# Two attention-and-feed-forward blocks on one core: cross-attention's first scores in whole steps, a last division two steps nearer, and the first mixture slot placed ahead of the last unit's norm

## The chip, the core and the metric

The kernel runs on one core of a Trainium2 chip. A core has five engines with a queue of instructions each: TensorE (PE; its weight loads are listed apart as PEld), VectorE (DVE), ScalarE (ACT), GpSimd (POOL) and SyncE (SP), which here issues most DMAs. Instructions of one engine start in the order of its queue, and wait for other engines by semaphores. Matmul results go to eight banks of PSUM; a bank can be written again when its reader is done. The metric is the device time of one execution in microseconds (us); a profiled execution adds the start and end of every instruction, and the share of full speed that TensorE's clock was granted.

## The reference, cut to what matters

Two blocks follow each other on x, 2 x 1024 tokens of width 256, 16 heads of 16:

```python
# block 0
q = _ln(latents); x = latents + _mha(q, q)                 # self-attention, 1024 keys
x = x + _mha(_ln(x), _ln(ctx))                             # cross-attention, 64 keys
h = _ln(x)                                                 # mixture: 8 experts, the best 2
vals, idx = top_k(h @ rw.T + rb, 2); gates = softmax(vals)
x = x + sum(gates * (gelu(h @ fc1[idx]) @ fc2[idx]))       # 256 -> 1024 -> 256
# block 1
x = x + softmax(q k^T * 0.25) v @ proj                     # self-attention, 1024 keys
x = x + softmax(q kc^T * 0.25 + bias(mask)) vc @ proj      # cross-attention, 64 keys, masked
x = x + gelu(_ln(x) @ fc1.T) @ fc2.T
```

All is in float32. Every softmax subtracts the row's maximum.

## The kernel before, in words

**Layers, cells, units.** A layer is one block. Its self-attention is written out as 128 cells: 2 batches x 8 steps "h" (two halves of the queries times four groups of four heads) x 8 blocks of 128 keys. A cell of `self_attention` computes, for four heads side by side in TensorE's rows, the scores of block "b" with the maxima subtracted (L969; ScalarE makes the exponentials, L947), and ten cells ahead the scores "a" from which VectorE takes the maxima (L937, four reduces of 128 x 512). Every one or two cells `product` (L1024) multiplies the exponentials with the values; ScalarE copies the result (L1036) and GpSimd adds it up (L1037). In the last ten cells there are no scores "a" left; then `maxima[0]` is false, and `helper()` gives such additions and other small work to VectorE instead of GpSimd.

A **unit** is 512 tokens; there are four in a layer. When a unit's self-attention is finished (`finish`), its row sums are inverted, turned through DRAM, spread and multiplied (`invert`, `turn_out`, `spread_out`, `divide` at L568, at set cells), and the projection (`project`, L492) is added to x. Then come, as tasks of a planner (`Stream`): the norm for cross-attention (`cnorm`, L381 to L412, L424), its queries (`ask`, L1295), its attention (`weigh`), its projection (`share`), and in layer 0 the mixture's `dispatch_task` of the unit: norm, router, top-2 choice, places, and eight indirect DMAs on GpSimd that scatter the rows by expert (L1676).

**The planner.** In each cell it advances "light" tasks by one step, up to a budget of about 1.1 us of assumed TensorE time, and in odd cells heavier tasks up to 2.2 us. A step says by `yield` how much TensorE time it takes (positive) or how long to wait until the next (negative). If more than 1.2 us of an odd cell stay free, the product of the cell before is made alone. After the last cell `rest` goes on by assumed time and rank. These figures only set the order in which instructions are written for TensorE, VectorE, ScalarE and SP; GpSimd's order is made by a scheduler.

**`weigh`.** While scores "a" still run (units 0 and 1 of each layer) it is a chain of 22 cells: eight half steps of first scores (`scores`, L1337, two banks each, two token tiles of four, with two reduces of 128 x 256 at L1345), `parts` (L1358) after each four, then `largest` (the maxima turned by TensorE, L1364), `weights` (scores again, minus the maxima, L1374 and L1380, exponentials L1385), `product` with the values and with ones for the sums, and the division through DRAM as above (`inverted`, `sent`, `brought`, `divided`, L1427). In layer 1 each bank begins with a matmul that adds the mask. Units 2 and 3 take another path, with whole steps and the division on TensorE (`undivided` L1434 and L1444, `division` L1459).

**The handover.** After layer 0's cells the experts' "slots" (256 rows of one expert: L1926 turns the rows, L1961 and L1967 the first layer, L1992 the second) begin. Slot 0 needs units 0 and 1 to be dispatched (`find(2)`, then `rows(2)`), slots 1 to 4 unit 2 (`find(3)`, `rows(3)`), the others unit 3. `find` searches on VectorE which expert and which rows a slot has; `load` issues weights (L1864) and rows (L1856) on the SP queue. Beside them run the keys and values of layer 1's context (L1207 to L1248), the last heads of unit 3 put together on TensorE (`side_by_side`, L880 to L906), and units 2 and 3 of cross-attention.

Of the kernel before, what the change touches and what calls it, by code (L numbers as in the profile page):

```python
# [51 lines left out]
P = 128  # L52
B, S, D, H, DH = 2, 1024, 256, 16, 16
SK = 64
# [181 lines left out]
def two_blocks(  # L236
# [17 lines left out]
    const = ctx.enter_context(tc.tile_pool(name="const", bufs=1))  # L254
# [24 lines left out]
    weights = {}  # L279
# [87 lines left out]
    maxima = [True]  # L367
# [213 lines left out]
    def self_attention(layer, tail, heads, arrive, extra, when_ready, beside=None):  # L581
# [7 lines left out]
        pools = ExitStack()  # L589
# [33 lines left out]
        QB, mx = {}, {}  # L623
# [217 lines left out]
        def finish(h, cell):  # L841


            b, qh, g = h // 8, h // 4 % 2, h % 4
            if g == 0:
                ot[b, qh] = opool.tile([P, 2, 512], F32, tag="ot", name=f"ot_{names}{b}{qh}")
            if layer == 0 and h >= 8 * B - 2:

                if g == 3:
                    stream.add(  # L850
                        side_by_side([acc.pop(h - 1), acc.pop(h)], ot[b, qh][:, 1, :]), 2.0,
                        mark="compact", rank=80,
                    )
                    project(b, qh, ["compact"])
                return
            if g % 2 == 0:
                sm = small.tile([P, 32], F32, tag="sums", name=f"sums_{names}{h}")
                sums[g // 2] = next_heads(), sm
            n, sm = sums[g // 2]
            dst = ot[b, qh][:, g // 2, :]  # L860
            send(acc.pop(h), n, g % 2, sm)
            if g % 2 == 1:
                by = opool.tile([P, 512], F32, tag="by", name=f"by_{names}{h}", bufs=1)
                gather(n, dst)
                slow = maxima[0]
                at_cell(cell + 1, lambda: invert(n, sm))
                at_cell(cell + 1 + slow, lambda: turn_out(n, sm))
                at_cell(cell + 2 + slow, lambda: spread_out(n, by))

                late = 3 + 2 * slow  # L870
                at_cell(cell + late, lambda: divide(dst, by))
                if g == 3:
                    at_cell(cell + late + 1, lambda: project(b, qh))
# [434 lines left out]
    def weigh(layer, b, pool, w, name, held):  # L1308
# [4 lines left out]
        q = held["ot"]  # L1313
        pts, pairs = {}, {}
        whole = maxima[0]
        mx = pool.tile([P, 2, 4, 4, 2], F32, tag="mxc", name=f"mx_{name}")
        turned_mx = []

        def scores(g, n, t0=0, nt=4):

            got = [(r, *bank()) for r in (2 * n, 2 * n + 1)]
            for r, _, p in got if layer == 1 else ():
                at = slice(32 * r, 32 * r + 1)
                nc.tensor.matmul(
                    p[:, : nt * P].rearrange("p (c k) -> p c k", k=SK),
                    lhsT=ones[at, :].bitcast(F32R),
                    rhs=mask_f[at, b * SK : (b + 1) * SK]
                    .bitcast(F32R)
                    .unsqueeze(1)
                    .to_broadcast([1, 2 * nt, SK]),  # L1330
                    start=True,
                    stop=False,
                )
            for t in range(nt):
                for r, _, p in got:
                    rows = slice(32 * r, 32 * r + 32)
                    nc.tensor.matmul(  # L1337
                        p[:, t * P : (t + 1) * P],
                        lhsT=q[rows, g, (t0 + t) * P : (t0 + t + 1) * P],
                        rhs=kbd[rows, g, b].rearrange("p u k -> p (u k)"),  # L1340
                        start=layer == 0,
                        stop=layer == 0 or t == nt - 1,
                    )
            for r, i, p in got:
                nc.vector.tensor_reduce(  # L1345
                    mx[:, g, r, t0 : t0 + nt, :].rearrange("p t u -> p (t u)"),
                    p[:, : nt * P].rearrange("p (c k) -> p c k", k=SK),
                    AX.X, ALU.max, negate=True,
                )
                free.append(i)  # L1350
# [119 lines left out]
        extra = 0.2 * layer  # L1470
        if whole:

            costs = {scores: 0.5 + extra / 2, largest: 0.9, weights: 1.1, product: 1.75}
            cells = [[] for _ in range(22)]
            for k in range(8):
                g, n, half = k // 4, k // 2 % 2, k % 2
                cells[k].append((scores, g, n, 2 * half, 2))
                if k % 4 == 3:
                    cells[k].append((parts, g))
            cells[9].append((largest,))  # L1480
            for g in range(2):
                for n in range(2):
                    cells[10 + 3 * g + (1 + g) * n].append((weights, g, (2 * n, 2 * n + 1)))
                at = 12 + 4 * g
                for after, step in ((0, product), (2, inverted), (2, sent), (3, brought), (5, divided)):
                    cells[at + after].append((step, g))
            for now in cells:
                for step, *args in now:
                    step(*args)
                us = sum(costs.get(step, 0.0) for step, *_ in now)  # L1490
                if us and now is cells[-1]:
                    yield us, None, True
                elif us:
                    yield us, 0.0
                elif now is not cells[-1]:
                    yield 0.0
            return
        costs = {scores: 1.0 + extra, largest: 0.9, weights: 1.2, undivided: 1.9, division: 0.55}
# [56 lines left out]
    def dispatch_task(unit, pool, counted):  # L1555
# [44 lines left out]
        mx = small.tile([P, 2, 4], F32, tag="mx2", name=f"mx2_{name}")  # L1600
        hots = [pool.tile([P, 4, E], F32, tag=f"hot{k}", name=f"hot{k}_{name}") for k in range(2)]
        for k in range(2):
            hot = hots[k]
            nc.vector.tensor_reduce(mx[:, k, :], lg, AX.X, ALU.max)
            nc.vector.tensor_tensor(hot, lg, mx[:, k, :].unsqueeze(2).to_broadcast(shape), ALU.is_equal)
            nc.vector.tensor_tensor(hot, hot, desc_b, ALU.mult)
            first = small.tile([P, 4], F32, tag="first", name=f"first_{name}{k}")
            nc.vector.tensor_reduce(first, hot, AX.X, ALU.max)
            nc.vector.tensor_tensor(hot, desc_b, first.unsqueeze(2).to_broadcast(shape), ALU.is_equal)
            yield -1.0  # L1610
            if k == 0:
                nc.vector.scalar_tensor_tensor(lg, hot, -3.0e38, lg, ALU.mult, ALU.add)
                nc.vector.tensor_scalar(
                    xd[:, :, D + M_E0], first, -1.0, float(E), ALU.mult, ALU.add
                )
# [17 lines left out]
        else:  # L1633
# [9 lines left out]
            pk, lhsT=ones, rhs=before.rearrange("p e t -> p (e t)"), start=False, stop=True  # L1643
# [20 lines left out]
        at = small.tile([P, 2, 4], U32, tag="at", name=f"at_{name}")  # L1664
        for k in range(2):
            mine = small.tile([P, 4, E], F32, tag="mine", name=f"mine_{name}{k}")
            nc.vector.tensor_tensor(mine, hots[k], place.rearrange("p e t -> p t e"), ALU.mult)
            nc.vector.tensor_reduce(at[:, k, :], mine, AX.X, ALU.max)
            yield -0.5
        counted()  # L1670

        for t in range(4):
# [133 lines left out]
    class Mixture:  # L1806
# [211 lines left out]
        def find(self, units):  # L2018

            last = units == len(NFULL)  # L2020
            had = self.places[-1].tiles if self.places else None
            end = NSLOT if last else NFULL[units]
            n = end - (self.ends[-1] if self.ends else 0)
            if units == 2:
                self.caps = expert_tiles("2", (FULL, ANY))
                caps = 2 * self.caps[:1]
            else:

                caps = [self.caps[last], *expert_tiles(f"{units}", (OVER, ANY) if last else (FULL,))]
            yield -0.9  # L2030
            pool = self.epool[1] if self.epool else const
            places = Places()
            yield from places.make(pool, f"{units}", n, had, caps, last)
            self.places.append(places)
            self.ends.append(end)
            yield 0.3
            yield -3.0

            self.load(1)
# [141 lines left out]
    def block(layer, tail, heads=None, beside=None):  # L2181

        pools = {}
# [6 lines left out]
        if layer == 0:  # L2190
            open_pools()
            context_places(0, pools["cpool"])
            choice(0, pools["cpool"])
            bias_out.extend(pools["dpool"].tile([P, D], F32, name=f"bias_out{i}") for i in range(2))
        made, ys, ready = [], [], {}

# [310 lines left out]
```

## Time and profile before

| | |
|---|---|
| median of 3 runs | 1526.23 us (1524.87 to 1527.06) |
| profiled execution | 1523.92 us, span 1522.0 us |
| mean granted clock of TensorE | 0.986 |
| TensorE busy | 1439.3 us, 95% |
| VectorE busy | 982.7 us, 65% |
| ScalarE busy | 919.9 us, 60% |
| GpSimd busy | 355.3 us, 23% |
| layer 0's self-attention | 63 us to 545 us |
| mixture, with layer 1's beginning | 573 us to 898 us |
| layer 1's self-attention | 898 us to 1375 us |

How to read it: the page gives the busy time of each engine, the span in 40 slices, DMA queues, the chain that ended last, and the costliest groups of instructions by line, operation and tiles. "L969" is line 969 of the kernel. Other views of the same trace give the busy time in chosen stretches, who waited for whom, and instructions in order of time; there the bracket behind an instruction is the time its engine was idle before it, and the releaser. A matmul in float32 stands as two records, one in the rounded form as one. Where the text prices a group of matmuls "start to start", it is the time from its first record to the first of the next group. The time of a cell is taken from the first of its four products with the ones row (qb_s, ones) at L969.

### The profile page before, as it was taken

The numbers are of one execution on the slowest core, as the hardware profiler recorded it, in microseconds if no ns is written. First come the engines' busy times: TensorE is split into PE (matmuls) and PEld (weight loads), VectorE is DVE, ScalarE is ACT, GpSimd is POOL, SyncE is SP. The second block draws the span as 40 slices with busy tenths as digits, with TensorE's granted clock in tenths as the row PEclk, the third lists the DMA queues.
The fourth block names the chain that finished last, engine by engine and source line by source line (L and its number), as shares of the span: only waits on it lengthen the run. The fifth ranks groups of instructions, "written<-read, shape, count | busy, mean of one in ns | idle before, by whom it ended". The sixth has DMA issues, their size and how long they took to land. (4 is left out here: it accounts for less than half of the span.)

```text
span 1522.0 us, 29849 instructions
## 1 busy us (share of the span) xinstructions
PE 1439.3 (95%) x11172; PEld 830.1 (55%) x11172; DVE 982.7 (65%) x2216; ACT 919.9 (60%) x1797; POOL 355.3 (23%) x488
## 2 busy tenths in 40 slices
PE   6999999999999977999999999999999999999998
PEld 3444444444434445788888664444454454446676
DVE  7867788869778665531115758877886886944210
ACT  3377788777777845323323347877877777783411
POOL 2221234225243122031112023211332322411010
PEclk9899999999999998999999999999999999999999
DMA  8653122111110030666566541132211112000000
GB/s 318 248 217 136 52 70 64 43 47 42 36 51 31 15 115 29 215 240 232 188 203 231 169 150 62 61 108 71 64 50 52 44 36 97 29 10 29 8 14 28
DMA packets 69157, 148.71 MB, mean 98 GB/s; under 512 B 12842, under 2 KB 26668, under 8 KB 68620
## 3 DMA queue, kind: packets, MB, share of 16 engines
q1 hardware_dynamic: 65788, 137.86, 26.6%
q0 software_dynamic: 3216, 8.85, 1.6%
q8 instruction: 91, 1.49, 0.4%
q14 instruction: 62, 0.51, 0.1%
HBM read 94.32 MB, written 51.99 MB: 96 GB/s over the span
## 5 line engine op out<-in xcount | busy, mean ns | idle before, releaser
L937 DVE TENSOR_REDUCE mx_s<-banks 128x1 f32<-128x512 f32 x1024 | 635.4, 683 | 131.2 <-PE banks L969 123.4
L947 ACT ACTIVATE pt_s<-banks 128x512 f32<-128x512 f32 x1024 | 535.2, 603 | 125.9 <-PE banks L969 120.1
L1024 PE MATMUL banks<-pt_s,v_s 128*18 128x512 f32 x2048 | 260.6, 603 | 9.6 <-ACT pt_s L947 5.4
L1037 POOL TENSOR_TENSOR acc_s<-acc_s,part_s 128x512 f32<-128x512 f32 x130 | 166.8, 1283 | 419.5 <-ACT part_s L1036 418.8
L969 PE MATMUL banks<-qb_s,ones 2*128 2x512 f32 x1024 | 200.6, 395 | 0.0
L1992 PE MATMUL banks<-w_slot,h_s 128*128 128x256 f32 x560 | 125.1, 380 | 0.4 <-DVE spread L1004 0.4
L1036 ACT COPY part_s<-banks 128x512 f32<-128x512 f32 x145 | 87.1, 601 | 48.0 <-PE banks L1024 42.6
L1992 PEld LDWEIGHTS banks<-w_slot,h_s 128*128 128x128 f32 x560 | 105.4, 190 | 15.6 <-DVE spread L1004 0.8
L1024 PEld LDWEIGHTS banks<-pt_s,v_s 128*18 128x18 f32 x2048 | 43.5, 97 | 126.8 <-ACT pt_s L947 66.4
L2001 DVE SCALAR_TENSOR_TENSOR ys<-banks,gate,b 128x256 f32<-128x256 f32 x35 | 16.9, 483 | 133.2 <-PE banks L1992 133.2
L969 PEld LDWEIGHTS banks<-qb_s,ones 2*128 2x128 f32 x1024 | 96.6, 186 | 8.9
L1967 ACT ACTIVATE h_s<-banks,w_slot 128x256 f32<-128x256 f32 (+1 forms) x104 | 41.1, 446 | 86.1 <-issue 48.3
L2007 POOL DMA_INDIRECT results<-ys,to x35 | 33.8, 966 | 224.3 <-DVE ys L2001 175.6
L1961 PE MATMUL banks<-xsT,w_slot 128*128 128x256 f32 (+1 forms) x416 | 84.9, 357 | 0.9 <-ACT xsT L431 0.9
L1961 PEld LDWEIGHTS banks<-xsT,w_slot 128*128 128x128 f32 x416 | 70.9, 190 | 12.0 <-issue 2.8
L2145 PE MATMUL banks<-hT_f,w_ff 128*128 128x512 f32 x128 | 57.0, 595 | 0.0
L2157 PE MATMUL banks<-w_ff,h_f 128*128 128x256 f32 x256 | 56.6, 379 | 0.0
L1345 DVE TENSOR_REDUCE mx_c<-banks 128x4 f32<-128x256 f32 (+1 forms) x96 | 44.2, 506 | 17.8 <-PE banks L1337 16.7
L698 PE MATMUL banks<-xT_s,w_att 128*128 128x512 f32 x104 | 50.9, 613 | 3.2 <-ACT pt_s L947 2.4
L1967 ACT ACTIVATE h_s<-banks,spare 128x256 f32<-128x256 f32 (+1 forms) x56 | 21.7, 444 | 51.1 <-PE banks L1961 34.9
L2157 PEld LDWEIGHTS banks<-w_ff,h_f 128*128 128x128 f32 x256 | 48.2, 190 | 7.2 <-issue 1.0
L2148 ACT ACTIVATE h_f<-banks,w_ff 128x512 f32<-128x512 f32 x32 | 21.9, 687 | 48.6 <-PE banks L2145 48.6
(376 smaller groups left out, 2926.8 us busy)
## 6 DMA issues: line engine op xcount, KB each, us to landing
w_slot<-in_ff_w_dram SPq DMA_DIRECT2D x40, 576.0 KB
sorted_rows<-fill SPq DMA_DIRECT2D x36, 520.0 KB
w_slot<-in_ff_w_dram SPq DMA_DIRECT2D x26, 514.0 KB
whole<-acc_s SPq DMA_DIRECT2D x30, 256.0 KB
spare<-in_ff_w_dram SPq DMA_DIRECT2D x14, 514.0 KB
q_parts<-spare SPq DMA_DIRECT2D x13, 512.0 KB
KS<-k_parts SPq DMA_DIRECT2D x12, 512.0 KB
k_parts<-spare SPq DMA_DIRECT2D x10, 512.0 KB
```

What stands on the lines that cost most here:

```text
L698: nc.tensor.matmul(p, lhsT=w[:, at + k * D + pair * P : at + k * D + (pair + 1) * P], rhs=xT[b][:, k, blk * 512 : (blk + 1) * 512], start= ...
L937: nc.vector.tensor_reduce(to, sc, AX.X, ALU.max)
L947: nc.scalar.activation(pt, sc, AF.Exp, scale=SCALE)
L969: nc.tensor.matmul(sc, lhsT=lhsT, rhs=rhs, start=now[0] == 1, stop=last)
L1024: nc.tensor.matmul(o[32 * j : 32 * j + VW, :], lhsT=V[b][:, cell % 8, 4 * g + j, :], rhs=exps.pop((cell, j)), start=(cell == cells[0]), st ...
L1036: nc.scalar.copy(part, o)
L1037: helper().tensor_tensor(acc[h], acc[h], part, ALU.add)
L1961: nc.tensor.matmul(ph[:, n, :], lhsT=w[:, at : at + P], rhs=xT[:, k, :], start=(k == 0), stop=(k == 1),)
L1967: nc.scalar.activation(h1[:, f, :rows], ph[:, n, :], AF.Gelu, bias=w[:, W_B1 + f : W_B1 + f + 1])
L1992: nc.tensor.matmul(py, lhsT=h1[:, f, h * P : (h + 1) * P], rhs=w[:, f * D : (f + 1) * D], start=(f == 0), stop=(f == 7),)
L2145: nc.tensor.matmul(ph, lhsT=w1[:, at : at + P], rhs=hT[:, k, :], start=(k == 0), stop=(k == 1))
L2157: nc.tensor.matmul(py[:, n, :], lhsT=h1[:, f, t * P : (t + 1) * P], rhs=w2[:, f * D : (f + 1) * D], start=(f == 0), stop=(f == 7),)
```

## The change

1. `scores` of `weigh` works on all four token tiles of a group at once. In the chain for units 0 and 1 four whole steps take the place of eight half steps, and the chain has 18 cells instead of 22: scores in steps 0, 1, 3 and 4 of the chain, maxima in 6, weights in 7, 8, 10 and 11, products in 9 and 12, the last division in 17.
2. In layer 0 the division of the heads with g = 3 (the last pair of a unit) is issued sooner after `finish`: the turn one cell after it instead of two, the spread after two instead of three, the multiplication after three instead of five, the projection after four instead of six.
3. In `dispatch_task` the first of the two rounds of the top-2 choice, and the first of the two rounds of places, no longer end in a pause once no scores "a" are left.
4. `find` may now be reached before the mixture's own pool exists; it then takes layer 0's `dpool`.

By 1 to 3 the planner reaches every later step of layer 0 sooner: unit 2's cross-attention starts at cell 106 instead of 110, and dispatch 1, `find(2)` and the projection of cross-attention of unit 2 are written in front of the end of the cells instead of behind it. Behind them slot 0's first instructions now stand in front of unit 3's norm, and the rows of slots 1 to 3 are loaded behind the weights of slots 1 and 2 and the first weights of slot 3 instead of behind those of slot 1 alone. In layer 1 the order differs only from cell 56 to cell 109.

```diff
             if g % 2 == 1:
                 by = opool.tile([P, 512], F32, tag="by", name=f"by_{names}{h}", bufs=1)
                 gather(n, dst)
-                slow = maxima[0]
+                slow = maxima[0] and (layer == 1 or g == 1)
                 at_cell(cell + 1, lambda: invert(n, sm))
                 at_cell(cell + 1 + slow, lambda: turn_out(n, sm))
                 at_cell(cell + 2 + slow, lambda: spread_out(n, by))
...
-        def scores(g, n, t0=0, nt=4):
+        def scores(g, n):
...
-                    .to_broadcast([1, 2 * nt, SK]),
+                    .to_broadcast([1, 8, SK]),
...
-            for t in range(nt):
+            for t in range(4):
...
             for r, i, p in got:
                 nc.vector.tensor_reduce(
-                    mx[:, g, r, t0 : t0 + nt, :].rearrange("p t u -> p (t u)"),
-                    p[:, : nt * P].rearrange("p (c k) -> p c k", k=SK),
+                    mx[:, g, r].rearrange("p t u -> p (t u)"),
+                    p.rearrange("p (c k) -> p c k", k=SK),
                     AX.X, ALU.max, negate=True,
                 )
...
-            costs = {scores: 0.5 + extra / 2, largest: 0.9, weights: 1.1, product: 1.75}
-            cells = [[] for _ in range(22)]
-            for k in range(8):
-                g, n, half = k // 4, k // 2 % 2, k % 2
-                cells[k].append((scores, g, n, 2 * half, 2))
-                if k % 4 == 3:
-                    cells[k].append((parts, g))
-            cells[9].append((largest,))
+            costs = {scores: 1.0 + extra, largest: 0.9, weights: 1.1, product: 1.75}
+            cells = [[] for _ in range(18)]
             for g in range(2):
                 for n in range(2):
-                    cells[10 + 3 * g + (1 + g) * n].append((weights, g, (2 * n, 2 * n + 1)))
-                at = 12 + 4 * g
+                    cells[3 * g + n].append((scores, g, n))
+                    cells[7 + 3 * g + n].append((weights, g, (2 * n, 2 * n + 1)))
+                cells[3 * g + 1].append((parts, g))
+                at = 9 + 3 * g
                 for after, step in ((0, product), (2, inverted), (2, sent), (3, brought), (5, divided)):
                     cells[at + after].append((step, g))
+            cells[6].append((largest,))
...
             nc.vector.tensor_tensor(hot, desc_b, first.unsqueeze(2).to_broadcast(shape), ALU.is_equal)
-            yield -1.0
+            if k == 1 or maxima[0]:
+                yield -1.0
...
             nc.vector.tensor_reduce(at[:, k, :], mine, AX.X, ALU.max)
-            yield -0.5
+            if k == 1 or maxima[0]:
+                yield -0.5
...
-            pool = self.epool[1] if self.epool else const
+            pool = self.epool[1] if self.epool else self.scratch
...
+            mixture.scratch = pools["dpool"]
```

More of the change, by code (lines that the diff above doesn't have):

```diff
@@ L1338, in scores @@
                         p[:, t * P : (t + 1) * P],
-                        lhsT=q[rows, g, (t0 + t) * P : (t0 + t + 1) * P],
+                        lhsT=q[rows, g, t * P : (t + 1) * P],
                         rhs=kbd[rows, g, b].rearrange("p u k -> p (u k)"),
                         start=layer == 0,
-                        stop=layer == 0 or t == nt - 1,
+                        stop=layer == 0 or t == 3,
                     )
@@ L1345, in scores @@
                 nc.vector.tensor_reduce(
-                    mx[:, g, r, t0 : t0 + nt, :].rearrange("p t u -> p (t u)"),
-                    p[:, : nt * P].rearrange("p (c k) -> p c k", k=SK),
+                    mx[:, g, r].rearrange("p t u -> p (t u)"),
+                    p.rearrange("p (c k) -> p c k", k=SK),
                     AX.X, ALU.max, negate=True,
```

## The prediction

> **What bounds the kernel now.** I read the page first (busy shares, the row of slices), then the busy time of each engine stage by stage, then what TensorE waits for, and last the SP queue where the first layer hands over to its mixture.
>
> ```profile
> PE 1439.3 (95%) x11172; PEld 830.1 (55%) x11172; DVE 982.7 (65%) x2216; ACT 919.9 (60%) x1797; POOL 355.3 (23%) x488
> ...
> PEclk9899999999999998999999999999999999999999
> ...
> L937 DVE TENSOR_REDUCE mx_s<-banks 128x1 f32<-128x512 f32 x1024 | 635.4, 683 | 131.2 <-PE banks L969 123.4
> ```
>
> TensorE is busy 95% of the span, so only its waits and its slow stretches can be won, unless work is removed. No matmul of weight is removed. In self-attention a cell with nothing beside it takes 2.69 us (from one cell's product with the ones row to the next's, 196 to 207 us), and four reduces at L937 take 4 x 0.683 = 2.73 us: VectorE is as full as TensorE there.
>
> The next view is the busy time of each engine in stretches; columns are the engines, then the granted clock, the DMA share and GB/s.
>
> ```profile
> 1107.17:1135.74 28.57, 28.11 (x321) 14.93 (x316) 25.75 (x53) 21.71 (x42) 7.73 (x6) 1.00 0.15 52
> ...
> 400.60:422.60 22.00, 18.70 (x206) 9.43 (x200) 20.53 (x49) 14.04 (x27) 5.12 (x4) 1.00 0.08 26
> 422.60:434.00 11.40, 10.10 (x78) 4.55 (x73) 8.41 (x24) 6.20 (x13) 1.82 (x2) 0.70 0.15 49
> 545.00:563.30 18.30, 17.43 (x142) 13.82 (x142) 13.78 (x57) 4.02 (x10) 8.35 (x9) 1.00 0.47 142
> 563.30:576.00 12.70, 2.82 (x12) 2.38 (x12) 11.43 (x52) 3.12 (x10) 2.63 (x2) 0.60 0.35 140
> ```
>
> Row one is a unit's eight half steps of first scores in layer 1 (cells 56 to 63): VectorE is 90% busy. Row two is cells 92 to 96 of layer 0, where the same steps of unit 1 meet the mixture's top-2 choice of unit 0: VectorE 93%, TensorE only 85%. Row three has the clock at 0.70. Row five is the handover after layer 0's attention: TensorE works 2.8 of 12.7 us and VectorE 11.4.
>
> What TensorE waits for, from its instructions in order of time (the bracket is the idle time before, and who ended it):
>
> ```profile
> 419.90 0.50 PE L969 MATMUL banks<-QS00h,KS 32*128 32x512 f32 x1 [1.66 <-DVE mx_c L1345]
> ...
> 424.61 0.83 PE L969 MATMUL banks<-KS,QS01h 32*128 32x512 f32 x2 [1.30 <-DVE mx_c L1345]
> ...
> 572.56 1.11 PE L424 MATMUL banks<-ident,xn_c 128*128 128x128 f32 x4 [9.35 <-DVE xn_c L412]
> ```
>
> Twice it waits for a bank that a cross-attention maximum still holds, and after the second the clock is at half from 425.8 to 432.6 us. At the handover it waits 9.35 us for the last unit's norm on VectorE, and the clock is at half from 565.7 to 576.0.
>
> **The change, part by part.**
>
> *Whole score steps.* The operation's own rows:
>
> ```profile
> L1345 DVE TENSOR_REDUCE mx_c<-banks x96: 408/418/692, 269.6 to 1421.9; 128x4 f32<-128x256 f32 x64, 128x8 f32<-128x512 f32 x32
> ```
>
> In each of four units (0 and 1 of both layers) 16 reduces of 256 become 8 of 512. Back to back, two of the first take 0.76 us (400.75) and two of the second 1.28 us (589.76): 8 x 0.76 - 4 x 1.28 = 1.0 us of VectorE less. The product with the mask in layer 1 falls from 16 to 8 matmuls of twice the width: nothing. Is the 1.0 us on the path? The eight cells took 28.57 us; TensorE alone would need 8 x 2.69 + 4 x 0.76 (64 matmul records of L1337, 16 of which take 0.76 us at 586.26) + about 1.2 (a transposed maximum of 0.66 and the mask) = 25.8; VectorE 32 x 0.683 + 6.1 + 0.8 = 28.8. So VectorE sets the stage. Bounds: 0 and 2.8 us a unit; I take 1.0, the work removed, **-4.0 us** for four. The weights and products now follow in six adjacent cells. Their TensorE time is the same, and ScalarE needs 4 x 0.52 for a cell's exponentials + 2 x 0.52 for the weights + 0.3 for half a copy = 3.4 us, against 2.69 + 0.65 = 3.3 on TensorE: bounds 0 and +0.5 a unit (six cells by 0.1), taken as 0, since two of the six carry a product of 2.2 us on TensorE.
>
> *The collision in layer 0.* Unit 0's dispatch starts 6 cells before unit 1's scores, in both kernels. Before, scores ran until the ninth cell and met the two top-2 steps (5 to 7 instructions of 0.19 us each, two of them 1.0 us beside GpSimd) and the count. Now they end with the sixth. Cells 92 to 96 took 22.0 us, and the same cells of layer 1, without a dispatch, 17.0 (1237.83 to 1254.81); 0.4 is the dispatch's own matmuls, so 4.6 us is waiting. In the new order the fifth to eighth cells want 17.1 us of VectorE and 13.3 of TensorE; about 1.3 us of lag is carried by the banks, so 2.5 us of waiting stay: **-2.0 us**, bounds 0 and -4.6.
>
> *The clock behind it.* 6.8 us at half speed cost 3.4 us. The remaining 2.5 us of waiting lie in some 14 us, less than 1 us in any 3.4 us. The trace's slow stretches come in steps of 3.41 us. 3.41 us with 1.30 (423), 1.32 (64), 1.45 (33) and 2.33 us (593) idle were followed by one, 3.41 us with 1.24 (576) and 0.91 us (607) were not. So it should go: **-3.4 us**, bounds 0 and -5.1 (with the 3.4 us at 285.8, which no idle time explains and which I leave). The Trainium skill, "TensorE: Matmul & The Clock Gate", section "HAM oscillation — how this bites in real kernels", gives the rule that only TensorE gaps over about 3.4 us matter. By it the waits of 1.66 and 1.30 us would not have slowed the clock, nothing would come back here, and the sum below would be -6.0 instead of -9.4. The slow stretches after 1.3 us decide for the trace.
>
> *Last division closer.* For pairs with g = 3 in layer 0 the transposition of the sums is issued one cell earlier, the multiplication two, the projection two. Three pairs, no instruction more. What hides it: before, heads 6 and 7 were multiplied by 321.8 us and projected from 331. The multiplication waited for its transfer from 316.7 to 320.5, so 4 us for the transfer and 1.3 for the work, against three cells (8 us) now. GpSimd adds queue behind it, with three buffers. 0, bounds 0 and +2. The new order also puts the eight scatters of dispatch 0 (1.27 us each, GpSimd) in one row ahead of two multiplications: inside that bound.
>
> *The handover.* Layer 0's units now run 4 cells earlier at the end. Dispatch 1, the search for slot 0 and cross-attention's projection of unit 2 move from behind the last attention product (544.85 us) to in front of it; slot 0 goes in front of unit 3's norm. Dispatch 1's four centred tiles go to GpSimd (4.84 us at 376 for dispatch 0's, against 1.38 on VectorE), two cells ahead of their transposes. Its eight scatters, 10.2 us, which waited from 544.98 for a memset behind the last product, run in GpSimd's idle tail, and the SP queue can load slot 0 from about t = 4 (before at 558.78, t = 14): its rows land by t = 14, needed at 17. TensorE's order from the last product on, priced by start-to-start times of before, with t = 0 there:
> - removed waits: 9.35 + 1.83 + 0.44 + 0.30 + 2.33 + 0.91 = 15.2 us, and 3.4 us for 6.8 us of work at half clock (572.6 to 576.0, 596.4 to 599.9);
> - added waits. The projection of unit 2 waits for its division, queued on VectorE behind two accumulations (0.69) and six small steps (1.1): 2.4 us. Slot 0's first matmul waits 1.2 us for ScalarE's copy of the turned rows (1.02). Dispatch 2's transposes come after two of slot 0's four groups, but their input stands on VectorE behind two sets of inverse roots (2.67 each), eight statistics (0.53 each), and slot 0's indices (1.3): 4.1 us. Small ones in its choice: 1.5. Unit 3's maxima share VectorE with the search for slots 1 to 4 (3.2 us between them): 3.6 us. Its exponentials have no slot beside them: 0.9. Together 13.7 us;
> - three of these are over 1.3 us, so the clock will dip; two dips of 3.4 to 6.8 us cost 3.4 to 6.8.
>
> The next fence is the SP queue of before, where slots 1 to 3 are loaded:
>
> ```profile
> 607.95 2.25 SPq L1864 DMA_DIRECT2D w_slot<-in_ff_w_dram  x4
> 610.77 2.21 SPq L1856 DMA_DIRECT2D xs<-sorted_rows  x3
> 613.49 0.91 SPq L1864 DMA_DIRECT2D w_slot<-in_ff_w_dram  x2
> 614.99 1.42 SPq L1864 DMA_DIRECT2D spare<-in_ff_w_dram  x2
> ```
>
> Before, the rows went after one slot's weights; now they stand behind ten transfers, 5.5 MB. At the 390 GB/s of 610 to 622 us that is 14 us from about t = 49, so the rows land near t = 65, and TensorE wants them at t = 61 without dips, 65 with them. So dips or rows, not both: +4.5. Sum of the handover: -15.2 - 3.4 + 13.7 + 4.5 = **-0.4 us**, with +0.5 for a fuller tail of attention **0**; bounds -6 (no dips, rows early) and +9.
>
> **Sum.** -4.0 - 2.0 - 3.4 + 0 = -9.4 us. The profiled execution took 1523.92 us (span 1522.0 and 1.9 around it), so 1514.5 on it. It lies 2.3 us under the median of the runs, 1526.23; on the median the forecast is **1517 us**.
>
> **Rivals.**
> - *Bursts throw the clock (slower).* A whole step puts 1.28 us on VectorE in one cell, and there are two pairs of steps in neighbouring cells in each of four units, eight in all. A pair wants 2 x (2.73 + 1.28) = 8.0 us of VectorE against 2 x (2.69 + 0.76) = 6.9 of TensorE: 1.1 us of waiting, close to the 1.3 that was followed by half clock. Against it: the banks carry 1.3 us of lag, and half steps made no dip in layer 1. If each pair costs 3.4 us of half clock, 8 x 1.7 = 13.6: -9.4 + 13.6 = +4.2, **1530 us**. It decides from six pairs on.
> - *Rows late (no change).* At 258 GB/s (the mean of 600 to 623) the 5.5 MB take 21 us, 7 more: -2.4, **1524 us**. The same time comes out if VectorE's 1.0 us and the dispatch's waits were hidden.
> - *The gap closes (much faster).* If waits at the handover after the change overlap better than I read them, -6 there and -1.7 for the dip at 286: **1509 us**.
>
> **How the numbers follow.** Forecast (1511 to 1522) 0.47, gap closes 0.10, no change 0.18, slower 0.25. About 0.2% (3 us) is what a measurement of this kernel can tell from no change. Faster: 0.47 + 0.10 = 0.57; same 0.18; slower 0.25. The likeliest case alone reaches from 1511 to 1522; the range over the cases from 1508 to 1531 leaves out half of the slower case and a little of the fastest, under 0.2.
>
> **What would show it.** Right: cells 56 to 63 of layer 1 about 1 us shorter, with 8 reduces of 512 a unit; no half clock between 390 and 440 us; no wait of 9 us after the last attention product, but three of 2 to 4 us. Wrong: half clock in layer 1's units; a wait on the rows of slot 1 over 6 us; waits at L1345 as long as now.

## The result: 1.3% slower, and the profile after

The changed kernel takes 1544.98 us (median of 4 runs, 1543.92 to 1548.31), the kernel before in the same group 1525.85 us (1524.87 to 1527.06): 1.0129 times as long, 95% interval 1.0111 to 1.0147. The forecast was 1517 us, so the sign is wrong. The profiled execution took 1544.2 us, its span 1542.4 us against 1522.0. It was run in two more groups, on two chips, each time beside the kernel before: 1.0064 and 1.0072 times as long.

The page of the changed kernel, the lines that answer to those shown of before:

```profile
PE 1451.9 (94%) x11156; PEld 831.5 (54%) x11156; DVE 972.7 (63%) x2165; ACT 912.8 (59%) x1786; POOL 355.9 (23%) x500
...
PEclk9999999999889998999999999999999999999999
...
L937 DVE TENSOR_REDUCE mx_s<-banks 128x1 f32<-128x512 f32 x1024 | 635.0, 681 | 145.4 <-PE banks L969 133.9
...
L1345 DVE TENSOR_REDUCE mx_c<-banks 128x8 f32<-128x512 f32 x64 | 40.9, 683 | 29.7 <-PE banks L1337 25.7
```

VectorE has 10.0 us less to do. About half of that is the reduces at L1345 (64 of 512 in place of 32 of 512 and 64 of 256, 4.9 us less in the sum of their durations); the rest is spread over small steps of the norms and the dispatch. VectorE waits 14.2 us longer in front of L937. TensorE is *busy* 12.6 us longer for the same work at a lower mean clock (0.980 against 0.986), and the row of slices has two eights in a row where layer 0's unit 1 is.

The table shows where the 20.4 us of the span went, by stages between the same instructions of both kernels; the part at half clock is in brackets. The fourth stage ends at the same matmul of slot 2's second layer (668.7 us before).

| stage | before, us | after, us | difference |
|---|---|---|---|
| start to cell 78 of layer 0 (unit 0) | 348.5 (13.7) | 345.2 (3.4) | -3.3 |
| cells 78 to 84 | 22.1 | 21.6 | -0.4 |
| cells 84 to 110 (unit 1, dispatch 0) | 106.0 (6.8) | 115.2 (27.3) | +9.3 |
| cell 110 to slot 2 (handover) | 192.2 (13.7) | 201.7 (23.9) | +9.6 |
| slot 2 to cell 54 of layer 1 | 430.7 (6.8) | 431.1 (6.8) | +0.4 |
| cells 54 to 78 (unit 0) | 88.0 | 90.3 | +2.3 |
| cells 86 to 110 (unit 1) | 88.5 | 90.6 | +2.1 |
| the rest of layer 1 | 246.1 (0.5) | 246.6 | +0.5 |

The stretches of the changed kernel (columns: length, busy time of the engines, granted clock, DMA share, GB/s): layer 1's cells 56 to 63; the half clock in layer 0; the handover up to the wait for dispatch 2's input, and that wait; and a stretch in unit 3's scores.

```profile
1122.62:1153.71 31.09, 29.16 (x316) 15.53 (x310) 25.61 (x47) 21.24 (x41) 5.12 (x4) 1.00 0.11 41
...
399.80:451.00 51.20, 46.42 (x322) 19.03 (x321) 30.39 (x74) 29.18 (x56) 13.08 (x12) 0.73 0.16 50
556.53:577.76 21.23, 18.40 (x109) 14.34 (x108) 13.70 (x55) 7.25 (x16) 0.53 (x1) 1.00 0.49 156
577.76:583.00 5.24, 0.01 (x1) 0.02 (x1) 4.37 (x25) 0.84 (x2) 0.00 (x0) 0.78 0.00 0
604.70:611.00 6.30, 2.89 (x12) 1.72 (x12) 1.71 (x8) 0.00 (x0) 3.66 (x4) 0.76 0.58 176
```

VectorE is 82% busy in the first row, where it was 90%: it has less to do and the stage is longer. The fourth row is a stall: TensorE does nothing for 5.2 us. In the last row TensorE starts only 12 records in 6.3 us, and VectorE works 1.7 us. In order of time (TensorE; idle time before and releaser in the bracket):

```profile
410.19 1.09 PE L1364 MATMUL banks<-ident,spread 128*128 128x128 f32 x4 [2.52 <-DVE lg_m L1610]
...
441.74 1.94 PE L1392 MATMUL banks<-pt_c,vbd 128*32 128x512 f32 x8 [1.93 <-ACT pt_s L947]
...
582.99 1.97 PE L424 MATMUL banks<-ident,xd_m 128*128 128x128 f32 x8 [5.23 <-DVE xd_m L1565]
...
605.89 0.26 PE L1337 MATMUL banks<-kbd,q_c 32*128 32x128 f32 x1 [0.21 <-issue]
606.62 0.36 PE L1337 MATMUL banks<-kbd,q_c 32*128 32x128 f32 x1 [0.47 <-issue]
607.34 0.26 PE L1337 MATMUL banks<-kbd,q_c 32*128 32x128 f32 x1 [0.36 <-issue]
...
627.41 1.53 PE L1925 MATMUL banks<-ident,xs 128*128 128x128 f32 x8 [2.54 <-DMA xs<-sorted_rows]
```

Single records of score matmuls start some 0.72 us apart and wait for nothing that the profile shows ("issue"). Otherwise such records start two by two, 0.1 us apart (from 602.30 us on in the same profile).

### The profile page after: what moved, and what is told of

The parts are those of the page before. It is cut to its first block, busy times and chain, and to the rows that moved or that the text cites. A ratio compares the mean times of both kernels' runs of the same rounds, so it can differ in the third digit from the quotient of the medians.

```text
span 1542.4 us, 29753 instructions
## 1 busy us (share of the span) xinstructions
PE 1451.9 (94%) x11156; PEld 831.5 (54%) x11156; DVE 972.7 (63%) x2165; ACT 912.8 (59%) x1786; POOL 355.9 (23%) x500
## 5 line engine op out<-in xcount | busy, mean ns | idle before, releaser
L937 DVE TENSOR_REDUCE mx_s<-banks 128x1 f32<-128x512 f32 x1024 | 635.0, 681 | 145.4 <-PE banks L969 133.9
L1037 POOL TENSOR_TENSOR acc_s<-acc_s,part_s 128x512 f32<-128x512 f32 x124 | 159.3, 1284 | 425.6 <-ACT part_s L1036 424.6
L1991 PEld LDWEIGHTS banks<-w_slot,h_s 128*128 128x128 f32 x560 | 106.4, 192 | 18.1 <-ACT h_s L1966 2.0
L1036 ACT COPY part_s<-banks 128x512 f32<-128x512 f32 x138 | 83.0, 602 | 47.8 <-PE banks L1024 45.5
L1345 DVE TENSOR_REDUCE mx_c<-banks 128x8 f32<-128x512 f32 x64 | 40.9, 683 | 29.7 <-PE banks L1337 25.7
L1966 ACT ACTIVATE h_s<-banks,spare 128x256 f32<-128x256 f32 (+1 forms) x56 | 21.6, 444 | 56.7 <-PE banks L1960 22.7
```

The source lines that it names most:

```text
L937: nc.vector.tensor_reduce(to, sc, AX.X, ALU.max)
L1036: nc.scalar.copy(part, o)
L1037: helper().tensor_tensor(acc[h], acc[h], part, ALU.add)
L1966: nc.scalar.activation(h1[:, f, :rows], ph[:, n, :], AF.Gelu, bias=w[:, W_B1 + f : W_B1 + f + 1])
L1991: nc.tensor.matmul(py, lhsT=h1[:, f, h * P : (h + 1) * P], rhs=w[:, f * D : (f + 1) * D], start=(f == 0), stop=(f == 7),)
```

## The experiments

Theory at the start ("density"): the chain of 18 cells puts more beside a cell than the banks carry, and waits follow, with half clock behind them. Rivals: the whole step itself ("burst"); the moved division and handover; the prediction's own sum, with layer 1 spoilt by what layer 0 left behind. Ratios are to the kernel before on the same chip.

### Which layer carries the loss

Whole steps and 18 cells in one layer alone, the chain of the other layer as before. In l1_only nothing else is changed; l0_only_SY has `layer == 0` in this place and the rest of the change.

```diff
+            if layer == 1:
+                costs = {scores: 1.0 + extra, largest: 0.9, weights: 1.1, product: 1.75}
+                cells = [[] for _ in range(18)]
...
+            else:
+                costs = {scores: 0.5 + extra / 2, largest: 0.9, weights: 1.1, product: 1.75}
+                cells = [[] for _ in range(22)]
...
```

> Whole score steps and the chain of 18 cells in layer 1 alone; layer 0, its last division and its handover as before. Theory 'density' (six adjacent cells of weights and products, and two whole steps in neighbouring cells, hold more than the banks carry): cells 56 to 77 and 88 to 109 of layer 1 take 82.5 and 83 us as in the changed kernel, where they took 80.2 and 80.7; +4.6, 1530.5 us, no half clock. Rival, the prediction's first step (the VectorE work saved is on the path, and what layer 1 lost in the changed kernel came from what layer 0 left behind): -2.0, 1524 us.

> The changed kernel with layer 1's units in half steps and 22 cells again; layer 0 as changed, with its whole steps, closer division and moved slot. If layer 1's two units carry the loss (1.9 to 2.3 us each by their cells, and half clock that follows score steps there), the rest is worth nothing: 0.998 to 1.002 times before, 6 to 9 us less than the changed kernel of this group. Rival (layer 0 carries it): 1.004 to 1.007, 4 to 5 us less.

Measured: layer 1 alone **1.0075** (1.0046 to 1.0105), median 1531.52 against 1521.60 us. Everything of the change but layer 1's steps: **1.0013** (0.9992 to 1.0033). Layer 1's two units, with layer 1 alone changed, and then with it as before:

```profile
1102.13:1184.60 82.47, 79.76 (x786) 37.99 (x780) 63.96 (x115) 61.44 (x119) 17.82 (x14) 1.00 0.14 47
1220.66:1306.51 85.85, 82.84 (x785) 38.70 (x780) 66.06 (x125) 61.53 (x119) 20.57 (x28) 0.96 0.16 57
```

```profile
1110.57:1190.76 80.19, 78.76 (x792) 38.52 (x788) 64.29 (x123) 62.29 (x121) 20.58 (x16) 1.00 0.15 47
1226.87:1307.75 80.88, 78.99 (x792) 38.52 (x788) 65.89 (x131) 62.40 (x121) 21.68 (x27) 1.00 0.17 60
```

The first unit is 2.3 us longer at full clock although layer 0 was untouched, so it is the own cost of the steps and their chain, and the prediction's own sum falls. The second is 5.0 us longer, 3.4 of it from 6.8 us at half clock. In these groups layer 1's two units carry the loss, by their cells and by half clock that comes with them.

### Whole step or dense chain

The kernel before with whole steps at every other cell of its 22 (w22):

```diff
...
-            for k in range(8):
+            for k in range(0, 8, 2):
...
-                cells[k].append((scores, g, n, 2 * half, 2))
+                cells[k].append((scores, g, n))
...
```

The changed kernel with two half steps in the cell of a whole one (h18_SY):

```diff
...
-                    cells[3 * g + n].append((scores, g, n))
+                    cells[3 * g + n].extend((scores, g, n, t0, 2) for t0 in (0, 2))
...
```

> Whole score steps in both layers, but at the first, third, fifth and seventh cell of a chain of 22 cells as before; weights, products, division and handover as before. Theory 'density': a whole step by itself costs nothing, and VectorE's 1.0 us a unit is won or hidden: 1522 to 1526 us, layer 1's units 79.2 to 80.2 us. Rival 'burst' (a reduce of 1.28 us for two banks is what holds TensorE up): layer 1's units at 81.5 us or more, more half clock than 6.8 us in layer 0's unit 1: 1530 us or more.

> The changed kernel with half steps again, two of them in each cell where it has a whole one: the same chain of 18 cells, the same order, only the reduces are 16 of 256 a unit again. Theory 'density': as slow as the changed kernel or by VectorE's 1.0 us a unit slower: 1545 to 1549 us. Rival 'burst': the half steps let the self-attention's maxima in between, 1526 to 1535 us.

Measured: w22 **1.0017** (0.9999 to 1.0036), h18_SY **1.0064** (1.0042 to 1.0086). Neither theory holds as put. Layer 1's second unit, cells 88 to 109 at full clock: 80.72 us before, 82.51 with whole steps spread over 22 cells (+1.8), 82.16 with half steps in 18 cells (+1.4), 82.83 with both (+2.1). So the whole step costs most of it even when spread, and two half steps in one cell, in the denser chain, cost nearly as much. Both have sixteen records of score matmuls in one cell, where before there were eight. This cost is read in the cells: the whole time of w22 is not clear of the kernel before, since its interval includes 1. VectorE's share of the eight cells 56 to 63 in w22:

```profile
1105.11:1135.45 30.34, 28.91 (x312) 13.58 (x306) 25.11 (x47) 21.63 (x42) 7.67 (x6) 1.00 0.13 44
```

0.64 us less work on VectorE than before, and 1.77 us more time. The waits in these eight cells (total, times, longest), before and then in w22:

```profile
ACT pt_s L947 <- PE banks L969: 4.0, 8, 0.8
...
DVE mx_c L1345 <- PE banks L1337: 2.3, 3, 1.1
...
PEld banks L969 <- DVE mx_c L1345: 1.1, 5, 0.3
```

```profile
ACT pt_s L947 <- PE banks L969: 7.6, 11, 1.4
DVE mx_c L1345 <- PE banks L1337: 4.7, 4, 1.7
...
PEld banks L969 <- DVE mx_c L1345: 3.8, 8, 0.6
```

VectorE waits twice as long for the scores of the step, then TensorE for the maxima, and ScalarE for the self-attention's scores that stand behind the step in TensorE's queue. The three take turns more and work side by side less. TensorE's idle time in the eight cells grows by 1.0 of the 1.77 us (28.57 less 28.11 before, 30.34 less 28.91 in w22); the other 0.8 us stands as busy time for no more work.

### What of a whole step does it

On w22, the maximum of the second bank one cell later, by a step of its own (w22_split):

```diff
...
                 cells[k].append((scores, g, n))
+                cells[k + 1].append((rest, g, n))
...
```

On w22, each bank's maxima in two reduces of 256 (w22_256):

```diff
+                for h in range(2 if whole else 1):
+                    m = nt // 2 if whole else nt
                     nc.vector.tensor_reduce(
-                        mx[:, g, r, t0 : t0 + nt, :].rearrange("p t u -> p (t u)"),
-                        p[:, : nt * P].rearrange("p (c k) -> p c k", k=SK),
+                        mx[:, g, r, t0 + h * m : t0 + h * m + m, :].rearrange("p t u -> p (t u)"),
+                        p[:, h * m * P : (h + 1) * m * P].rearrange("p (c k) -> p c k", k=SK),
                         AX.X, ALU.max, negate=True,
                     )
...
```

The kernel before with eight steps in the same eight cells, each of one bank and all its columns (onebank):

```diff
...
-                cells[k].append((scores, g, n, 2 * half, 2))
+                cells[k].append((scores, g, n, 0, 4, (k % 4,)))
```

> Whole score steps at every other cell of a chain of 22 cells, in both layers, but the maximum of the second bank is taken one cell later than that of the first: 0.68 us of VectorE beside each cell instead of 1.28 beside every second; the matmuls stay in one row. In the same chain with both maxima in one cell, layer 1's units took 1.8 to 1.9 us more than with half steps. Theory 'two maxima in a row': back at 80.2 us a unit or under, 0.998 to 1.000. Rival 'matmuls in a row' (VectorE finds nothing to do while TensorE makes two whole banks of scores, and the self-attention's scores come late): still 1.5 us or more.

> The same chain of 22 cells with whole score steps and both banks' maxima in one cell, each in two reduces of 256 instead of one of 512 (1.0 us a unit more on VectorE). If the wide reduce is what is slow: layer 1's units back at 80.2 us. If the block is (matmuls and maxima of two banks in a row): 82 to 83 us, 1.002 to 1.004.

> The kernel before, with each half step (two banks, half their columns) replaced by a step of one bank and all its columns: eight steps in the same eight cells, 8 reduces of 512 a unit. Theory 'block' (a whole step is slow because VectorE waits until TensorE has filled two banks, and TensorE then waits until VectorE has emptied them; the width of the reduce is not the cause): layer 1's units at 79.2 to 80.2 us, 2 to 4 us less than before in all. Rival (TensorE needs two row groups side by side, or the reduce of 512 is the cause): units at 81.5 us or more, 4 us more than before.

Measured: w22_split **1.0045** (1.0030 to 1.0061), w22_256 **1.0021** (1.0010 to 1.0032), onebank **1.0079** (1.0053 to 1.0105). Cells 56 to 63 of layer 1 in the three, in this order:

```profile
1109.06:1139.48 30.42, 29.25 (x312) 13.73 (x308) 26.03 (x45) 21.52 (x42) 7.69 (x6) 1.00 0.12 43
```

```profile
1103.03:1133.91 30.88, 28.93 (x313) 13.59 (x306) 25.65 (x55) 21.62 (x42) 7.67 (x6) 1.00 0.13 43
```

```profile
1105.67:1141.50 35.83, 34.87 (x313) 19.46 (x309) 25.97 (x47) 21.73 (x42) 7.79 (x7) 0.90 0.12 42
```

As the rivals of the first two had it: 30.34, 30.42 and 30.88 us against 28.57 before. Neither maxima one after the other nor a wide reduce is what costs; the time stays when they are taken apart. What the three share is the row of sixteen records of score matmuls (and two mask products of 512) between two cells' scores. That this row is the cause is argued, by elimination and from the waits; it was not taken away by itself. Steps of one bank, which by the theory "block" should have won, are the slowest: 88.4 us for the first unit, 5.1 of the extra 8.2 us from 10.2 us at half clock, and 3.1 from the form of the step. A likely source of the 3.1 us stands in the traces. The eight records of a half step, on two row groups, start two by two within 0.34 us (from 1110.38 in the kernel before); those of a step of one bank start one after the other over 0.78 us (from 1108.99 in onebank). That is 0.44 us more of TensorE's time in each of eight cells, or an estimated 3.5 us. Its row is also as long as that of a whole step (0.79 us for sixteen records in w22), so the run does not speak against the row as the cause. What starts the half clock there stays open.

### The moved division and handover

The edits for the division and the two pauses, with half steps and 22 cells:

> The changed kernel with the half steps and the chain of 22 cells of before: only the last division closer and the search for a slot without its two pauses stay, so that layer 0's units start two cells earlier. If the chain of 18 cells is the cause of the whole loss: 1523 to 1528 us. Rival (the moved dispatch, division and handover cost by themselves): 1531 to 1536 us, with the time lost between layer 0's cell 120 and the second slot.

Measured: **1.0001** (0.9984 to 1.0017). Together they neither cost nor win, and the profile shows a gain and a loss: cell 110 of layer 0 starts at 469.6 us instead of 476.5 (10.2 us of half clock until then instead of 20.5, which is worth some 5 us), and the stage from there to slot 2 is 3.1 us longer. TensorE in front of slot 1, and the SP queue:

```profile
613.45 1.97 PE L1928 MATMUL banks<-ident,xs 128*128 128x128 f32 x8 [10.09 <-DMA xs<-sorted_rows]
```

```profile
593.28 5.34 SPq L1866 DMA_DIRECT2D w_slot<-in_ff_w_dram  x8
599.20 0.87 SPq L1866 DMA_DIRECT2D spare<-in_ff_w_dram  x2
602.42 12.67 SPq L1858 DMA_DIRECT2D xs<-sorted_rows  x4
```

The rows stand behind ten weight transfers, as the prediction's rival had it, and TensorE waits 10.1 us for them, where the kernel before has no such wait. In the changed kernel the same wait was only 2.5 us. So the order was changed: `did` (a slot's half is finished) loads no weights of a further slot while only slot 0's rows are known.

```diff
                 self.done[half] += 1
-            self.load()
+            self.load(NSLOT if self.nrows > 1 else 0)
```

> The kernel with the last division closer and the search without its two pauses, half steps in 22 cells as before, and the rows of slots 1 to 3 ahead of all weights but one slot's. Without that last edit TensorE waited 10.1 us for slot 1's rows, and the time was that of the kernel before. Theory 'rows': 8 to 10 us less than before, 0.994 times. Rival (weights or slot choice come late in place of the rows): 0.998 to 1.001.

> The changed kernel, with the rows of slots 1 to 3 ahead of all weights but one slot's in the SP queue. If rows behind weights and the 5.5 MB in flight beside unit 3's scores hold TensorE up there (the stretch at 605 to 611 us, and 2.5 us at slot 1): 8 us less than the changed kernel. Rival (the stretch has nothing to do with the transfers): 1 to 3 us less.

Measured: SY_rows **0.9935** (0.9910 to 0.9960), median 1514.29 against 1523.40 us. **This version beats both kernels** of its group: the handover's two edits and the order of rows, with half steps kept. The changed kernel with the same order of rows: 1.0031 (1.0010 to 1.0051), beside 1.0064 without in the same group; its wait for slot 1's rows (1.7 us there) is gone and the stage to slot 2 is 3.2 us shorter. That is near the rival's 1 to 3 us, and since no stretch of single matmuls stood there without the edit either, the run says nothing on that stretch. The whole times of these two kernels differ by less than their intervals can tell apart. TensorE and the SP queue in SY_rows:

```profile
612.04 1.80 PE L1928 MATMUL banks<-ident,xs 128*128 128x128 f32 x8 [2.70 <-DMA xs<-sorted_rows]
```

```profile
599.26 2.58 SPq L1866 DMA_DIRECT2D w_slot<-in_ff_w_dram  x4
607.29 2.16 SPq L1858 DMA_DIRECT2D xs<-sorted_rows  x3
609.95 2.89 SPq L1866 DMA_DIRECT2D w_slot<-in_ff_w_dram  x4
```

The wait falls from 10.1 to 2.7 us, and the stage from cell 110 to slot 2 from 195.3 to 187.5 us (192.2 in the kernel before). Each of the two edits alone, with the rows' order:

> The kernel before with the last division closer and the rows of slots 1 to 3 ahead of all weights but one slot's; the search for a slot keeps its two pauses, so that slot 0 stands behind the last unit's norm. If slot 0 in front of that norm is what won 9 us with both edits: 0.998 to 1.001. If the earlier division and start of layer 0's units won it: 0.993 to 0.996.

> The kernel before with the search for a slot without its two pauses and the same order of rows; division as before, and slot 0 behind the last unit's norm, since the units start no earlier. Alone it moves the slot by too little: 0.998 to 1.001. Rival (the pauses are what is won): 0.993 to 0.996.

Measured: closer division **0.9969** (0.9953 to 0.9984), pauses alone 0.9991 (0.9981 to 1.0001), both 0.9935. The result for the division lies between the two theories: with the order of rows, its earlier units win some 0.3% without slot 0 in front of the norm. That this slot, which needs both edits, wins as much again is not shown: "both" comes from another chip and another group, the two intervals overlap (0.9953 to 0.9960), and the profiled execution with the division alone is the shorter (span 1510.5 against 1514.6 us). The order of rows was not tried without either edit.

### The changed kernel again

> The changed kernel itself, next to the others of this group. If whole steps in a chain of 18 cells are what cost twice as much as half steps in the same chain: 1.012 to 1.014 times the kernel before, cells 84 to 110 of layer 0 at 112 us or more and layer 1's units 2.2 us longer. If much of the difference to the half steps was a matter of one execution (TensorE's single matmuls 0.72 us apart at 605 to 611 us): 1.006 to 1.009, and no such stretch.

> The changed kernel a third time. It was 1.0129 times the kernel before at first (with 6 us of single matmuls in unit 3's scores at 605 to 611 us, and 27 us at half clock in layer 0's cells 84 to 110) and 1.0064 the second time (without the former, and with 10 us). If the first was a matter of single executions or of that chip: 1.005 to 1.009 again and neither stretch. If the kernel has two ways to run on any chip: some times near 1.013 among these.

Measured: **1.0064** (1.0042 to 1.0085) and **1.0072** (1.0047 to 1.0096). Cells 84 to 110 took 106.5 and 106.4 us (10.2 us at half clock), the stage to slot 2 194.0 and 194.3, and no stretch of single matmuls was there. Layer 1 repeats but for the clock: cells 56 to 77 of its first unit took 82.51 and 84.11 us, cells 88 to 109 of its second 84.46 and 82.77, and each time the longer one had 3.4 us at half clock. So 1.0129 is the loss of the first group, and about half of it is not the kernel's on every chip: half clock in cells 84 to 110 (20.5 us more than before, worth 10 us) and the stretch at 605 to 611 us. What started these is not settled. The weights did not start the stretch: after the record at 604.47 us the next starts at 605.19, and SP issues the slots' weights only at 607.51 us:

```profile
607.51 10.51 SPq L1863 DMA_DIRECT2D w_slot<-in_ff_w_dram  x8
```

A 16 KB transfer of the instruction queue begins at 604.74 us, but in the two repeats one begins at 593.75 and 592.96 us, as late in the same row of scores, and no such stretch follows.

## Why the prediction was wrong, step by step

- **Whole score steps, -4.0: wrong, and the step that failed.** The prediction took VectorE to set the stage and its saved work to come off the time. That rested on a sum of 28.8 us of VectorE's work beside 28.57 us measured, and the sum added durations that overlap. Four reduces in a row take 2.48 us and not 4 x 0.683 = 2.73:

```profile
196.49 2.48 DVE L937 TENSOR_REDUCE mx_s<-banks 128x1 f32<-128x512 f32 x4 [0.21 <-PE banks L969]
```

The 0.21 us before them is VectorE waiting in a cell of 2.69 us, so it was not as full as TensorE even there. In the eight cells it was busy 25.75 of 28.57 us, and TensorE 28.11, where the prediction's sum had 25.8. VectorE had 2.8 us to spare, so it did not follow that work taken from it comes off the time. What the runs showed in its place: VectorE's work fell (25.75 to 25.11 us in w22), and the eight cells grew by 1.77 us, 1.8 us a unit. The order in which TensorE's work and its waits follow had a price, and the prediction put it at nothing. Its bounds, "0 and 2.8 us a unit" of gain, excluded a loss without a reason. In layer 0 the first unit's cells 52 to 78 took 95.8 to 95.9 us in the three profiles of the changed kernel, and 94.5 with half steps in 22 cells and all else alike (SY).

- **Six adjacent cells of weights and products, 0 (at most +0.5 a unit): inside the bound.** With whole steps, packing 22 cells into 18 adds 0.3 us (82.51 to 82.83). Half steps in 18 cells cost 1.4 us a unit, but that includes two steps in one cell.
- **The collision in layer 0, -2.0, and the clock behind it, -3.4: wrong.** TensorE's idle time in cells 84 to 110 did fall in the two repeats (6.7 to 5.4 us), 1.3 of the 2.0; in the first run it rose to 7.6, with 2.52 us in front of L1364 and 1.93 in front of L1392. No run shows the 1.3 us of lag that the sum lets the banks carry. The half clock stayed (10.2 us in the repeats, 27.3 in the first run, where 6.8 were to go). The rule that under 1.3 us idle is safe failed: the half clock from 399.8 us follows 3.41 us with 0.19 us idle.
- **Last division, 0: inside its bound or a little better.** Cells 52 to 78 of layer 0 took 94.5 us with it and half steps, and 96.7 before with 1.7 of that from half clock.
- **The handover, 0 (bounds -6 and +9): the mechanism was right.** The wait of 9.35 us is gone. Waits that were to come did: 2.4 for unit 2's division (1.5 measured), 1.2 for slot 0's turned rows (0.66), 4.1 for dispatch 2's transposes (5.23), 3.6 for unit 3's maxima (3.8 in the repeats). In the repeats the stage took 194.0 and 194.3 us, in six kernels with the old order 192.2 to 194.7: no difference that these tell apart. Half clock came, and more than forecast: 20.5 us behind the cells, where two dips of 3.4 to 6.8 us were expected. In the first run the stage was 9.6 us longer, just outside the bound. The half clock in the whole stage, 23.9 us, was the same in all three; what the repeats did not have are 3.5 us more in cells 110 to 127, with 3.4 more of half clock, and the single matmuls, which no step of the prediction had.
- **Rivals.** "Rows late" happened in full where nothing else held TensorE up first (10.1 us); the 390 GB/s from which it was reckoned are 377 in the trace. "Bursts throw the clock" had the right sign, by luck in part: in the first run layer 1's units had no half clock at all, and in the repeats one unit each had 3.4 us. It was to come from 1.1 us of waiting; in the step before it TensorE was idle 0.2 us. The rival also had -4.0 still in its sum; its +4 us is half of what the later groups show (+9) and a fifth of the first. "The gap closes" needed the rows ahead of the weights: then the handover's edits win 9 us, with half steps kept.

## What to carry to other kernels

- Add up an engine's work from busy time in a stretch and not from durations that overlap; the row that showed 25.75 us stood beside the sum of 28.8. Here two engines, 90% and 98% busy, fed each other, and fewer, larger steps cost time although they saved work. Bound such an edit by a loss too, and try the size of the step by itself.
- When a stage is brought forward, look at what is now issued ahead of the data that it needs. Here one condition on the order of loads stands between 1.0001 and 0.9935, each from one group.
- A small step that a planner moves shifts everything behind it; build each part alone before adding up parts.

## What the runs showed of the hardware that was not expected

**Half clock with little idle time.** The clock record of the 16 profiles was cut into its 3.41 us steps, from 34 us after the start to the last matmuls. Counted are steps at full clock, by TensorE's idle time in them, and how many were followed by half clock; the last three rows go by the records of score matmuls (L1337) that start in the step:

| in the step before | steps | followed by half clock |
|---|---|---|
| 2.0 us idle or more | 37 | 37 |
| 1.3 to 2.0 us | 39 | 23 |
| 1.0 to 1.3 us | 45 | 13 |
| 0.7 to 1.0 us | 95 | 8 |
| under 0.7 us, 12 or more records of L1337 | 298 | 33 |
| under 0.7 us, 1 to 11 | 240 | 3 |
| under 0.7 us, none | 5978 | 5 |

So 1.3 us is no threshold but about even odds. Steps with a row of these matmuls (32 of 128 rows, 128 columns, a weight load each) were followed by half clock in 11% of cases, those without in 0.1%, while TensorE was idle for under 0.7 us in both. In layer 1's units none of 12 with half steps over 22 cells met half clock, and 9 of 20 with any of the other forms did. The Trainium skill, "TensorE: Matmul & The Clock Gate", section "HAM oscillation — how this bites in real kernels", gives the rule that TensorE should have no idle gaps over about 3.4 us; in these profiles far shorter ones were followed by half clock, so that rule alone does not describe them. What of these matmuls the clock goes by was not tried, nor whether it is they or something that goes with them.

**Groups differ.** The same pair of kernels gave 1.0129, 1.0064 and 1.0072 in three groups; the interval of the first meets neither of the others. The kernel before itself had medians from 1521.07 to 1525.85 us. Half a per cent here is to be read only beside the partner on the same chip, and a size from more than one group. Most ratios above are from one group.
